# Decoder layer on one core: operands of two quarters in one load, small transfers joined, output products spread, DVE in program order

## The chip, the cores and the metric

One core of a Trainium2 chip runs the whole program in one launch. The metric is device time in microseconds, from the first to the last instruction with what lies around them. The engines are PE (matrix products), DVE (vector), ACT (activations and scaled copies), POOL (elementwise) and SP, which here only issues transfers between main memory and the on-chip memory. Products land in the PSUM banks, of which there are eight.

## The reference

Eight sequences of 512 tokens with 256 features pass through three sublayers, each followed by a layer norm without gains.

```python
x = _layernorm(x + _L0_attn_ref(x, w_qkv, w_proj))           # self-attention, 16 heads of 16, rotary
x = _layernorm(x + _L0_xattn_ref(x, ctx_1024, ctx_1024, Wq, bq, Wk, bk, Wv, bv, Wo, bo))  # cross-attention, 16 heads
x = _layernorm(x + _L0_ffn_ref(x, wqkv, q_scale, k_scale, wo, ln_g, ln_b, w1, b1, w2, b2))
```

The third sublayer is itself a stack of two layers, each with local attention in windows of 128 tokens (8 heads of 64, unit-length queries and keys, a rotary table with a decay, a look at the window before) and a gated network of 682 hidden features after a layer norm:

```python
for l in range(2):
    x = _layer(x, wqkv[l], q_scale[l], k_scale[l], wo[l], ln_g[l], ln_b[l], w1[l], b1[l], w2[l], b2[l])
```

All is float32. The kernel gets this accuracy by writing each operand as a high part and a low part in a shorter format and adding three products (high by high, high by low, low by high).

## The kernel before

**Stages.** Sixteen items (`seq`: eight sequences of self-attention, then eight of cross-attention) take four quarters each, a quarter being four heads. They are the first stage, 64 quarters. Then come 64 windows of local attention (two layers of 32), with the gated network's halves (`half`) between them.

**Who sets the order.** Each function registers pieces of work with a planned time: `pe(...)` for products, `at(...)` at a time, `af(...)` so long after a product. `tq(q, g, u)` is the planned start of quarter q (plus g quarters and u sixteenths of it), with `TQ` microseconds to a quarter. `trace()` replays the plan, taking a PSUM bank's reuse as `GAP` behind its last product, sorts all pieces by time and emits them. `ORDERED` names the engines whose instructions are tied to this order (PE and ACT). For DVE, POOL and SP a scheduler beneath chooses, after the first microseconds. Each engine and each transfer queue works through its own list strictly in order, so what waits holds up what stands behind it.

**A quarter** (`quarter`). `fill` brings the operands of four heads from main memory (`dh`) into a half of `kA` or `kB` (keys) and one of four `Qst` tiles (queries), as four transfers of 192 KB. Two quarters ahead, sixteen products `pss` give scores whose row maxima DVE takes (`mx`, tile `nm`). `nhl` on POOL splits the maxima in two parts, `pm` on PE transposes them, ACT copies them (`mhl`) and two small transfers (`mq`) set them as two more rows under the queries, so that sixteen more products `pst` give scores less maximum, transposed. ACT takes their exponentials (`ex`, tile `pt`), and products `po` with the values and a column of ones give output and sums. On PE this is a chain of blocks: four `pst` and four `pss`, four `po`; in the middle of each block stands a filler.

**Fillers** are the products of other items: queries and keys (`project`, three products at a time), values (`values`, six), and the output projection (`end`, tile `pp`, six). They share one PSUM bank, "m". Their places are given by the numbers `K0`, `K1`, `Q0`, `Q1`, `V0`, `V1`, `E0` and `E1` in sixteenths of a quarter from the item's first quarter. An output projection of one half (256 tokens) is followed by two adds on DVE (`res`), statistics, a reciprocal root on ACT and POOL, a scaled copy and a store.

**Normalizing** (`norm`). ACT copies `po` to `ob`, SP stores it (`od`). Every second quarter `norm` runs six parts, at `n0` to `n5` microseconds after the last `po`: load of sums (`sm`) and outputs (`OTr`), reciprocal on DVE (`rs`), its way through main memory (`rd`, `R`), a multiplication and a split on POOL.

**Weights of the windows** (`pre_weights`, `pre`). Beside cross-attention 34 tiles are loaded (`f_w`), split on POOL and stored in two transfers (`spl`); `fetch` brings them back later. `small_loads`, `xp_load` and `xp_scale` bring biases, gains, scales and the rotary tables `xp` and multiply the tables by the scales. `low_zeros` writes zeros under the low key parts `kLA` and `kLB`, which serve only the windows.

Of the kernel before, what the change touches and what calls it, by code (L numbers as in the profile page):

```python
# [10 lines left out]
F32 = mybir.dt.float32  # L11
# [16 lines left out]
NC2 = 72  # L28
TQ = 13.05
TW = 13.49  # L30
GAP = 0.7
# [4 lines left out]
    'hne': 1, 'fne': 1, 'nw4': 1, 'gce': 0, 'f2': 1.5, 'f3': 2.514, 'E0z': 120, 'E1z': 124, 'nd': 3,  # L36
    'phx': 0, 'psf': 2.0, 'np': 2, 'nhe': 1, 'pa': 9.182, 'pb': 36.0, 'pst0': 0.75, 'pr': 4.9,
    'px0': -6.0, 'px1': 0.5, 'pcut': 8.255, 'wvt': 8.0, 'wpt': 50.0, 'v0': 5.801, 'pmz': 3.4, 'acq':
    0.543, 'trt': -0.482, 'so_': 0, 'ld': 0.024, 'ct': -0.049, 'ath': 0.3, 'acp': 0.34, 'ra': 1.2,
    'rb': 3.612, 'c0': 6.101, 'c1': 0.771, 'cl': 0.9, 'sh': 1.043, 'sl': 3.159, 'avc': 0.269, 'rs':  # L40
    0.001, 'rb_': -0.03, 'ead': 0.4, 'est': 1.802, 'fi': 0.202, 'mh': 0.122, 'md': 1.2, 'mq': 4.283,
    'ob': 0.522, 'od': 1.2, 'n0': 4.069, 'n1': 7.425, 'n2': 8.487, 'n3': 11.192, 'n4': 14.127, 'n5':
    14.896, 'wl': 0.698, 'sp': 1.2, 'spl': 0.8, 'wr': 0.299, 'ws': -0.192, 'h1': 6.196, 'hb': 6.5,
    'hh': 0.422, 'hl': 1.056, 'LB': 1, 'x1': 9.0, 'rk': 7.466, 'rq': 6.0, 'sd': 17.807, 'pt':
    18.326, 'nw': 6, 'bx': 3, 'en': 2, 'ea': 0.404, 'eb': 0.722, 'pvg': 1, 'run': 2, 'phe': 0,
    'xke': 1, 'ohe': 1, 'pvn': 4, 'trx2': -0.174, 'q2': 0.027, 'k2': -0.077, 'v2': 0.0, 'tq2':
    -0.215, 'tk2': -0.339, 's2': 0.137, 'p2': 0.011, 'w2': 0.186, 'm2': 0.043, 'mn': 7, 'K0': -100,
    'K1': -92, 'Q0': -84, 'Q1': -76, 'V0': -56, 'V1': -48, 'E0': 124, 'E1': 132, 'T0': -120, 'T1':
    -92, 'nh': 1.6, 'pm': 7.854, 'mp': 0, 'trx': 0.61, 'xh': 0.93, 'xl': 2.343, 'q': 0.307, 'k':
    -0.038, 'sq': -0.05, 'sum': 1.287, 'rn': 3.235, 'un': 3.706, 'r0': 4.857, 'r1': 5.838, 'v':  # L50
    0.585, 'vc': 0.574, 'tq': 0.119, 'tk': -0.15, 'qh': 0.659, 'ql': 1.085, 's': 0.406, 'ds': 0.111,
    'ma': -0.055, 'so': 1.814, 're': 2.218, 'no': 4.347, 'p': 0.056, 'dp': 0.174, 'pc': 0.514, 'pv':
    0.201, 'oh': -0.155, 'ol': 1.273, 'w': 0.192, 'dw': 0.083, 'wa': 0.94, 'th': 0.761, 'g0':
    -0.359, 'g1': 1.888, 'm': 0.375, 'dm': 0.095, 'mad': -0.105, 'pe': 6, 'ne': 13, 'h': 0.618, 'f':
    0.484, 'mx': -0.083, 'ex': 0.488, 'pq0': 0, 'pq1': 5, 'lq': 22.263, 'ldq': 3.16, 'pcd': 3.053,
    'sq_': 0, 'pst': 8.62, 'nw1': 1, 'nw3': 1, 'nd1': 0.437, 'ne1': 0.395, 'nd3': 0.525, 'tp':
    -0.271, 'tpd': -0.102, 'lw1': 1.125, 'lw2': 0.37,
}
P.update({'ws': 0.5, 'T1': -100, 'trt': 0.2})

# [3 lines left out]
def tile_decoder(  # L64
# [5 lines left out]
    f_w, f_qs, f_ks, f_gb, f_b1, f_b2,  # L70
# [11 lines left out]
    drp = ctx.enter_context(tc.tile_pool(name="drp", bufs=3, space=DRAM))  # L82
    dr1 = ctx.enter_context(tc.tile_pool(name="dr1", bufs=1, space=DRAM))
# [68 lines left out]
    ORDERED = ("PE", "Activation") + ("SP",) * P['so_']  # L152
# [17 lines left out]
    def trace():  # L170
# [49 lines left out]
        steps.sort(key=lambda s: s[:3])  # L220
        for t, _, _, fn in steps:
            fn()
            ins = nc.cur_bb.bb.instructions
            for i in ins[seen[0]:]:
                e = str(i.engine).split(".")[-1]
                if e not in ORDERED and t > T0 + P['pt']:
                    continue
                if e in last:
                    tc.add_manual_dep(
                        i, last[e],  # L230
                        mybir.DependencyInfo(mybir.DependencyClass.NoSync, mybir.DependencyReason.DATA),
                        reason="order",
                    )
                last[e] = i.name
            seen[0] = len(ins)
# [123 lines left out]
    NST = 4  # L359
    kA, kB, kLA, kLB = [stk.tile([128, NW, 4, 128], F32R, name=f"kT{i}") for i in range(4)]  # L360
    Qst = [stk.tile([128, 2, N], F32R, name=f"Qst{i}") for i in range(NST)]
# [18 lines left out]
    def setup_keys():  # L380

        for k in (kA, kB):
            for r in (48, 112):
                dma(k[r:r + 2].rearrange("p w g n -> p w (g n)").bitcast(F32),
                    ones.unsqueeze(1).to_broadcast([2, NW, N]))
# [13 lines left out]
    def att_weights(kind, t0, dt):  # L399
# [4 lines left out]
        for c in range(2):  # L404
            r = slice(c * 128, c * 128 + 128)
            if kind == 0:
                parts = lambda r=r: [(lambda f: f, s_wqk[r])]
            else:
                parts = lambda r=r: [(lambda f: f[:, :256], c_wq[r]), (lambda f: f[:, 256:], c_wk[r])]
            load_split(t0 + c * dt, "wqk", parts, le, W, ("qk", c), q=qs[c])  # L410
        for n, (key, src) in enumerate((("v", (s_wv, c_wv)[kind]), ("p", (s_wp, c_wo)[kind]))):
            hook = None
            if kind == 1 and key == "p":
                hook = out_bias
            load_split(t0 + (2 + n) * dt, "w" + key,
                       lambda src=src: [(w2d, src.rearrange("(c p) m -> p c m", p=128))],
                       lv, W, key, q=qs[n], hook=hook, **({} if kind else {"dt": P[('wvt', 'wpt')[n]]}))
# [348 lines left out]
    def quarter(q):  # L766
# [3 lines left out]
        Q = Qst[q % NST]  # L770
        Sq = {}

        def fill():
            ks = (kA, kB)[q // 2 % 2].rearrange("p w g n -> p (w g n)")
            Kt[q] = [ks[:, (q % 2 * 2 + g) * N:(q % 2 * 2 + g) * N + N] for g in range(2)]
            behind("dh", i, 0, 4 if q else 0)
            for t, d in ((ks[:, q % 2 * 2 * N:q % 2 * 2 * N + 2 * N], dhs[1]), (Q.rearrange("p g n -> p (g n)"), dhs[0])):
                for e in range(2):
                    dma(t[e * 64:e * 64 + 48].bitcast(F32).rearrange("p (g n) -> p g n", g=2),
                        d[i % ND][4 * qd + e:4 * qd + 4:2].rearrange("g r n -> r g n"))  # L780
            Sq["nm"] = sp.tile([128, 4, NW], F32, name="nm", tag="nm")

        at(tq(q - 3, 2, P['fi']) if q else T0 + 13.0, fill)


# [40 lines left out]
        def mq():  # L826
            m = Sq.pop("mhl")
            for par in range(2):
                dma(Q[par * 64 + 48:par * 64 + 50].bitcast(F32).rearrange("r g (c n) -> r (g c) n", c=NW),
                    m[par * 16:par * 16 + 16])  # L830
# [49 lines left out]
        af(e_, P['od'], od)  # L880
        if qd % 2:
            for part, d in enumerate((P['n0'], P['n1'], P['n2'], P['n3'], P['n4'], P['n5'])):
# [28 lines left out]
    def xp_load(l):  # L911
# [3 lines left out]
        for j, s in enumerate((f_qs[l:l + 1], f_ks[l:l + 1])):  # L915
            t = W["xp"][j].rearrange("p (t w d) -> p t w d", t=2, w=NW)
            dma(qk[:, 2 * j], s.to_broadcast([128, 64]))
            dma(qk[:, 2 * j + 1, 0:32], s[:, 32:64].to_broadcast([128, 32]))
            dma(qk[:, 2 * j + 1, 32:64], s[:, 0:32].to_broadcast([128, 32]))
            for a in range(2):  # L920
                dma(t[:, a], t_xp[2 * j + a].rearrange("(w p) d -> p w d", p=128))
# [21 lines left out]
    def pre(t, l, key, load, gain=None, tail=False):  # L943
# [4 lines left out]
        def cut(part):  # L948
# [5 lines left out]
            elif part == 1:  # L954
                h, lo = st["h"] = c2("wsh", F32R), c2("wsl", F32R)
                nc.gpsimd.tensor_copy(h, f)
            else:
                h, lo = st["h"]
                sub(nc.gpsimd, lo, f, h)

        def store():
            dma = (dma_, dma_g)[P['sq_']]
            h, lo = (a.bitcast(F32) for a in st.pop("h"))
# [7 lines left out]
            else:  # L971
                dma(d[0], h)
                dma(d[1], lo)
# [29 lines left out]
    def pre_weights():  # L1003
        n = NL * len(TILES)
        ta, tb = tq(4 * B + P['pq0']), tq(8 * B - P['pq1'])
        for l in range(NL):
            at(tq(4 * B) if l == 0 else tq(4 * B, 1), held(lambda l=l: small_loads(l)))
# [16 lines left out]
    def small_loads(l):  # L1024
        W = MW[l]
        gb = W["gb"] = const.tile([128, 2, 2], F32, name=f"gb{l}")
        dma(gb, f_gb[l])
        b1 = W["b1"] = const.tile([128, 11], F32, name=f"b1{l}")
        dma(b1, f_b1[l])
        b2 = W["b2"] = const.tile([128, D], F32, name=f"b2{l}")  # L1030
        dma(b2, f_b2[l:l + 1].to_broadcast([128, D]))
# [335 lines left out]
    def half(hb):  # L1367
# [97 lines left out]
        def gate(c, part):  # L1465
# [14 lines left out]
            if c < 4:  # L1480
                u = Qst[c].rearrange("p g n -> p (g n)")[:, hb % 2 * N:hb % 2 * N + N]
# [95 lines left out]
    at(T0 + 60.0, low_zeros)  # L1577
# [16 lines left out]
def layout(inputs):  # L1594
# [22 lines left out]
    for k, n in (("f_qs", "q_scale"), ("f_ks", "k_scale"), ("f_b2", "b2")):  # L1617
        a[k] = f(g["L0_ffn_" + n])
    nl = a["f_b2"].shape[0]
# [17 lines left out]
    a["f_gb"] = f(np.stack([g["L0_ffn_ln_g"], g["L0_ffn_ln_b"]], 1).reshape(nl, 2, 2, 128).transpose(0, 3, 1, 2))  # L1637
# [7 lines left out]
    a["f_b1"] = b1  # L1645
# [13 lines left out]
    for m in (sc, 1.0 / sc):  # L1659
        tb.append(np.concatenate([c * m, c * m], axis=1))  # L1660
        tb.append(np.concatenate([-s * m, s * m], axis=1))
    a["t_xp"] = np.stack(tb).astype(np.float32)
# [7 lines left out]
         "c_bv", "c_bo", "f_w", "f_qs", "f_ks", "f_gb", "f_b1", "f_b2", "t_cs", "t_xp", "t_mask"]  # L1670
# [17 lines left out]
```

## Time and profile before

| | |
|---|---|
| median of three runs | 2227.28 us (2225.7 to 2239.14) |
| profiled execution | 2240.65 us, its span 2238.9 us |
| mean granted clock of PE | 0.966 |
| PE busy | 2134.8 us, 95% |
| ACT, DVE, POOL busy | 1687.5, 1648.9, 1469.2 us |
| moved by transfers | 324.92 MB, mean 145 GB/s |
| time per quarter, between `pm` products | 12.6 to 23.8 us from the ninth quarter to the fifty-eighth, 11.2 where no filler stands |

The profile shows one execution. Busy shares are means over stages that differ: what a hole in an engine is worth must be read in its stage. A line of the timeline gives start, duration, engine, source line, operation, the tiles that it writes and reads, how many, and in brackets how long the engine stood idle before it and what ended that. Many products are issued from one helper (L244), so they are told apart by tiles. "PEld" is the loading of the standing operand, which runs beside PE. A PE that is busy is not a PE at its peak, and its speed depends on the granted clock.

### The profile page before, as it was taken

The page shows a single profiled execution, that of the slowest core. Times are in us where ns is not written, and L with a number is a line of the kernel's source. Part 1 is how long each engine was busy: PE and PEld are TensorE (multiplying, and loading weights), DVE is VectorE, ACT ScalarE, POOL GpSimd, SP SyncE. Part 2 cuts the span into 40 slices and gives each one's busy share as a digit, 9 for nine tenths or more (in the row PEclk, how much of TensorE's full clock was granted, in tenths as well). Part 3 has the DMA queues.
Part 4 walks back from the last instruction along what each step waited for, and adds up shares of the span by engine and source line. Part 5 has one row for each costly group of instructions (what it writes and reads, how often), then busy time and mean ns, then how long its engine had stood idle before and what let it go on. Part 6 is the DMA issues. An engine that isn't in the chain of part 4 may idle for free.

```text
span 2238.9 us, 46438 instructions
## 1 busy us (share of the span) xinstructions
PE 2134.8 (95%) x15016; PEld 1528.5 (68%) x15016; DVE 1648.9 (74%) x4126; ACT 1687.5 (75%) x4087; POOL 1469.2 (66%) x2052
## 2 busy tenths in 40 slices
PE   8999999999999999998999999999999999999996
PEld 6434444444444444367889999998989898989986
DVE  4878888877787768826777777776777777777773
ACT  2778888877787778846878777787777878787874
POOL 5276666324565546347777777777778888888874
PEclk7899999999999999979999999999999999999998
DMA  7566666656778777555433333334453333333331
GB/s 185 147 204 182 196 191 197 197 163 207 225 248 252 243 251 244 175 152 153 120 84 86 86 89 87 84 86 136 105 165 88 96 94 89 87 97 91 92 89 42
DMA packets 249734, 324.92 MB, mean 145 GB/s; under 512 B 41756, under 2 KB 131956, under 8 KB 249492
## 3 DMA queue, kind: packets, MB, share of 16 engines
q1 hardware_dynamic: 248788, 320.90, 50.4%
q8 instruction: 121, 1.98, 0.4%
q10 hardware_dynamic: 704, 1.05, 0.1%
q14 instruction: 121, 0.99, 0.1%
HBM read 156.24 MB, written 110.36 MB: 119 GB/s over the span
## 4 chain that ended last, share of the span: by engine, by line
PE 74%; DMA 9%; ACT 6%; POOL 5%; DVE 4%; issue 2%; SPq 1%; POOLq 0%; ACTq 0%; DVEq 0%
PE pga L244 11%; PE pst L244 10%; PE po L853 10%; PE pqkv L244 9%; PE pqk L244 4%; PE po L244 4%; PE pss L244 4%; PE py L244 4%; PE plo L1300 4%; PE pls L244 3%; PE ptp L1284 3%; PE pv L244 2%; PE ptr L1179 2%; DMA hs<-xd 2%; PE pp L244 2%
## 5 line engine op out<-in xcount | busy, mean ns | idle before, releaser
L796 DVE TENSOR_REDUCE nm<-pss 128x1 f32<-128x512 f32 x1024 | 653.2, 683 | 194.7 <-PE pss L244 152.5
L845 ACT ACTIVATE pt<-pst 128x512 f32<-128x512 f32 x1024 | 556.8, 602 | 139.1 <-PE pss L244 87.0
L244 PE MATMUL pst<-Qst,kT 50*128 50x512 f32 x1024 | 392.7, 461 | 22.7 <-ACT pt L845 13.7
L244 PE MATMUL pss<-kT,Qst 48*128 48x512 f32 x1024 | 399.3, 470 | 11.4 <-DVE nm L796 8.8
L244 PEld LDWEIGHTS pst<-Qst,kT 50*128 50x128 f32 x1024 | 164.5, 191 | 278.3 <-ACT pt L845 212.1
L244 PE MATMUL pqkv<-fwqh,xwT 128*128 128x512 f32 x768 | 311.7, 414 | 1.4 <-ACT pt L845 1.4
L853 PE MATMUL po<-pt,Vst 128*32 128x512 f32 x2048 | 284.1, 628 | 0.0
L1248 ACT ACTIVATE ms<-ms,n 128x256 f32<-128x256 f32 (+1 forms) x512 | 241.2, 473 | 41.7 <-DVE n L1240 36.2
L244 PE MATMUL pga<-hTh,w1h 128*128 128x256 f32 x704 | 204.1, 290 | 0.3 <-ACT hTh L1426 0.3
L1144 POOL TENSOR_TENSOR rT<-qn,xp 128x256 f32<-128x256 f32 x256 | 182.7, 735 | 31.6 <-DVE qn L1134 22.5
L244 PE MATMUL pga<-hTl,w1h 128*128 128x256 f32 x704 | 200.1, 284 | 1.5 <-DVE hTl L266 1.4
L1259 POOL TENSOR_TENSOR ms<-ms,lrs 128x512 f32<-128x512 f32 (+1 forms) x192 | 180.6, 947 | 31.1 <-DVE lrs L1254 24.8
L1240 DVE CUSTOM_DVE_ANT_0 ms<-pls,mask 128x256 f32<-128x256 f32 (+1 forms) x512 | 175.5, 383 | 33.4 <-PE pls L244 31.3
L244 PE MATMUL pga<-hTh,w1l 128*128 128x256 f32 x704 | 199.2, 283 | 0.0
L244 PEld LDWEIGHTS pss<-kT,Qst 48*128 48x128 f32 x1024 | 165.6, 192 | 28.5 <-DVE nm L796 20.4
L1474 ACT ACTIVATE gg<-pga,b 128x256 f32<-128x256 f32 (+1 forms) x192 | 91.2, 475 | 120.9 <-PE pga L244 117.5
L244 PE MATMUL pls<-kT,qs 128*128 128x256 f32 (+1 forms) x1024 | 168.8, 287 | 5.4 <-DVE n L1240 2.8
L1151 POOL TENSOR_TENSOR qn<-qn,xp 128x512 f32<-128x512 f32 x128 | 165.2, 1291 | 10.0
L1153 POOL TENSOR_TENSOR qn<-qn,rT 128x512 f32<-128x512 f32 x128 | 165.3, 1291 | 9.9
L244 PEld LDWEIGHTS pqkv<-fwqh,xwT 128*128 128x128 f32 x768 | 148.1, 193 | 24.1 <-ACT pt L845 2.4
L244 PE MATMUL pqkv<-fwql,xwT 128*128 128x512 f32 x384 | 154.1, 401 | 0.0
L244 PEld LDWEIGHTS pls<-kT,qs 128*128 128x128 f32 x1024 | 142.1, 192 | 11.1 <-issue 2.8
(172 smaller groups left out, 5502.9 us busy)
## 6 DMA issues: line engine op xcount, KB each, us to landing
kT<-kh SPq DMA_DIRECT2D x256, 128.0 KB
dh<-phi SPq DMA_DIRECT2D x60, 512.0 KB
kT<-dh SPq DMA_DIRECT2D x128, 192.0 KB
Qst<-dh SPq DMA_DIRECT2D x128, 192.0 KB
od<-ob SPq DMA_DIRECT2D x64, 256.0 KB
kT<-kl SPq DMA_DIRECT2D x128, 128.0 KB
dh<-plo SPq DMA_DIRECT2D x60, 256.0 KB
wst<-f_w SPq DMA_DIRECT2D x46, 256.0 KB
```

Source lines behind the costliest of these rows:

```text
L244: nc.tensor.matmul(out_, a, b_, start=i == 0, stop=i == n - 1)
L796: nc.vector.tensor_reduce(Sq["nm"][:, hh, qc:qc + 1], Sq.pop(("s", u)), AX.X, ALU.max, negate=True)
L845: nc.scalar.activation(p, Sq.pop(("t", hh)), AF.Exp, scale=scale)
L853: nc.tensor.matmul(po[hh * 32:hh * 32 + 32, :], V[kc][:, h * 17:h * 17 + 32], Sq.pop(("p", kc, hh)), start=kc == 0, stop=kc == NW - 1)
L1144: nc.gpsimd.tensor_tensor(h8(T2)[:, :, a * 32:a * 32 + 32], h8(qn)[:, :, 32 - a * 32:64 - a * 32], xp[:, 1, w:w + 1, a * 32:a * 32 + 32].t ...
L1151: nc.gpsimd.tensor_tensor(h8(qn), h8(qn), xp[:, 0, w:w + 1].to_broadcast([128, 8, 64]), ALU.mult)
L1153: nc.gpsimd.tensor_tensor(qn, qn, R.pop(("T2", j)), ALU.add)
L1240: nc.vector.tensor_tensor_reduce(ms[:, m, :nk], ps[:, m, :nk], FW[0]["mask"][:, 256 - nk:], -8.0, 3.0e38, ALU.add, ALU.min, n8[:, m:m + 1])
L1248: nc.scalar.activation(ms[:, m, :nk], ms[:, m, :nk], AF.Exp, bias=n8[:, m:m + 1], scale=-1.0, accum_out=sm[:, m:m + 1])
L1259: nc.gpsimd.tensor_tensor(pr[:, :, :nk], pr[:, :, :nk], rs.unsqueeze(2).to_broadcast([128, 2, nk]), ALU.mult)
L1300: nc.tensor.matmul(po[par * 64:par * 64 + 64, g * 128:g * 128 + 128], V[:, h * 64:h * 64 + 64], PT[:, par, c], start=c == 0, stop=c == nch ...
L1474: nc.scalar.activation(S["g", c][:rows], gin, AF.Gelu, bias=gb)
```

## The change

Operands: the four loads of a quarter become four of 384 KB for a pair of quarters (from the third quarter on), and there are three places for a pair instead of two. `kLA` and `kLB` serve as keys and queries of the third, and so `low_zeros` moves from the start to the end of the first stage.

Small transfers: the two stores of a split weight become one (from a tile of its own in a pool `wsp`; the common pool shrinks from 72 to 68 tiles), and biases, gains, scales and rotary tables are laid out by the host so that 26 small loads become 8.

Output products: `E0` and `E1` go from 124 and 132 to 108 and 124, and the K, Q and V places and other planned times move with them. Splitting of the window weights begins at quarter 15.4 instead of 32.

Order: DVE is tied to the program's order until the last quarter of the first stage (`do_` 1); the reciprocal and its neighbours are planned later (`n0` to `n5`), except for the last item.

```diff
-TQ = 13.05
+TQ = 12.91
-GAP = 0.7
+GAP = 0.49
...
-    ... 'ob': 0.522, 'od': 1.2, 'n0': 4.069, 'n1': 7.425, 'n2': 8.487, 'n3': 11.192, 'n4': 14.127, 'n5': 14.896
-    ... 'K0': -100, 'K1': -92, 'Q0': -84, 'Q1': -76, 'V0': -56, 'V1': -48, 'E0': 124, 'E1': 132, 'T0': -120, 'T1': -92
+    ... 'ob': 0.522, 'od': 1.367, 'n0': 5.72, 'n1': 9.555, 'n2': 10.595, 'n3': 13.85, 'n4': 18.602, 'n5': 22.869
+    ... 'K0': -108, 'K1': -100, 'Q0': -92, 'Q1': -76, 'V0': -60, 'V1': -52, 'E0': 108, 'E1': 124, 'T0': -112, 'T1': -100
+    ... 'pqa': 0.482, 'do_': 1, 'po_': 0
...
-    ORDERED = ("PE", "Activation") + ("SP",) * P['so_']
+    ORDERED = ("PE", "Activation")
+    ORDERED_A = ORDERED + ("SP",) * (P['so_'] == 1) + ("DVE",) * (P['do_'] == 1) + ("Pool",) * (P['po_'] == 1)
...
-                if e not in ORDERED and t > T0 + P['pt']:
+                if e not in (ORDERED_A if t < t_att else ORDERED) and t > T0 + P['pt']:
...
-    Qst = [stk.tile([128, 2, N], F32R, name=f"Qst{i}") for i in range(NST)]
+    Qst = [stk.tile([128, 4, N], F32R, name=f"Qst{i}") for i in range(2)]
+    KR = [t.rearrange("p w g n -> p (w g n)") for t in (kA, kB, kLA)]
+    QR = Qst + [kLB.rearrange("p w g n -> p (w g n)").rearrange("p (g n) -> p g n", n=N)]
...
         def fill():
-            for t, d in ((ks[:, q % 2 * 2 * N:q % 2 * 2 * N + 2 * N], dhs[1]), (Q.rearrange("p g n -> p (g n)"), dhs[0])):
-                for e in range(2):
-                    dma(t[e * 64:e * 64 + 48].bitcast(F32).rearrange("p (g n) -> p g n", g=2),
-                        d[i % ND][4 * qd + e:4 * qd + 4:2].rearrange("g r n -> r g n"))
+            n = 1 if q < 2 else 2
+            lo, hi = q % 2 * 2, q % 2 * 2 + 2 * n
+            for t, d in ((KR[r].rearrange("p (g n) -> p g n", n=N), dhs[1]), (QR[r], dhs[0])):
+                for e in range(2):
+                    dma(t[e * 64:e * 64 + 48, lo:hi].bitcast(F32),
+                        d[i % ND][4 * qd + e:4 * qd + 4 * n:2].rearrange("g r n -> r g n"))
...
-        at(tq(q - 3, 2, P['fi']) if q else T0 + 13.0, fill)
+        if q < 2 or q % 2 == 0:
+            at(tq(q - 3, 2, P['fi']) if q else T0 + 13.0, fill)
+        at(tq(q - 3, 2, P['fi']) if q else T0 + 13.0, begin)
...
-        for j, s in enumerate((f_qs[l:l + 1], f_ks[l:l + 1])):
-            t = W["xp"][j].rearrange("p (t w d) -> p t w d", t=2, w=NW)
-            dma(qk[:, 2 * j], s.to_broadcast([128, 64]))
-            dma(qk[:, 2 * j + 1, 0:32], s[:, 32:64].to_broadcast([128, 32]))
-            dma(qk[:, 2 * j + 1, 32:64], s[:, 0:32].to_broadcast([128, 32]))
-            for a in range(2):
-                dma(t[:, a], t_xp[2 * j + a].rearrange("(w p) d -> p w d", p=128))
+        dma(qk.rearrange("p t d -> p (t d)"), f_qk[l:l + 1].to_broadcast([128, 256]))
+        for j in range(2):
+            dma(W["xp"][j], t_xp[j])
...
-                dma(d[0], h)
-                dma(d[1], lo)
+                dma(d.rearrange("a p n -> p a n"), hl)
...
-        ta, tb = tq(4 * B + P['pq0']), tq(8 * B - P['pq1'])
+        ta, tb = tq(4 * B * P['pqa'] + P['pq0']), tq(8 * B - P['pq1'])
...
-    at(T0 + 60.0, low_zeros)
+    at(tq(4 * L - 4, 2), low_zeros)
```

## The prediction

> **What bounds the kernel now.** I read the page first, then busy time by stretches, then the timeline of each engine around every hole in PE.
>
> ```profile
> span 2238.9 us, 46438 instructions
> PE 2134.8 (95%) x15016; PEld 1528.5 (68%) x15016; DVE 1648.9 (74%) x4126; ACT 1687.5 (75%) x4087; POOL 1469.2 (66%) x2052
> PEclk7899999999999999979999999999999999999998
> ```
>
> PE bounds it; the others stand at 66 to 75%. So a change can pay in two ways only: fewer holes in PE, or fewer stretches at a lower granted clock. By stretches (us, then busy time of PE, PEld, DVE, ACT, POOL, then granted clock, DMA share, GB/s):
>
> ```profile
> 134.00:450.00 316.00, 309.19 (x1916) 134.94 (x1914) 256.32 (x450) 259.02 (x531) 190.46 (x265) 1.00 0.66 194
> 450.00:892.00 442.00, 417.01 (x2474) 187.69 (x2472) 329.04 (x583) 338.37 (x686) 222.40 (x351) 0.95 0.74 229
> 892.00:985.00 93.00, 84.79 (x478) 38.04 (x474) 54.13 (x104) 65.58 (x135) 37.17 (x53) 0.94 0.62 181
> 985.00:1080.00 95.00, 84.43 (x562) 72.79 (x559) 56.45 (x196) 60.23 (x182) 62.73 (x93) 0.87 0.52 146
> 1080.00:1540.00 460.00, 455.57 (x3707) 420.62 (x3705) 351.60 (x1070) 361.12 (x981) 349.38 (x445) 1.00 0.34 86
> 522.40:532.70 10.30, 10.10 (x38) 4.16 (x39) 5.42 (x10) 3.71 (x7) 4.12 (x6) 0.50 0.68 221
> ```
>
> Self-attention (134 to 450) runs at full clock, cross-attention (450 to 892) at 0.95, the window stage from 1080 on has 1% of holes. The loss is in cross-attention and at the seam behind it. The last line shows what a hole costs besides itself: after one, the clock is 0.50 for about 10 us. The hole and its makers, from the timelines:
>
> ```profile
> 514.50 0.33 SPq L238 DMA_DIRECT2D od<-ob  x1
> 519.46 0.66 SPq L238 DMA_DIRECT2D sm<-od  x1
> 521.64 0.35 DVE L692 RECIPROCAL rs<-sm 128x32 f32<-128x32 f32 x1 [3.87 <-DMA sm<-od]
> 522.60 0.79 PE L244 MATMUL pss<-kT,Qst 48*128 48x512 f32 x1 [3.30 <-DVE nm L796]
> ...
> 728.99 0.64 SPq L238 DMA_DIRECT2D sm<-od  x1
> 730.34 0.68 SPq L238 DMA_DIRECT2D Qst<-mhl  x1
> 734.30 0.76 PE L244 MATMUL pst<-Qst,kT 50*128 50x512 f32 x1 [1.72 <-DMA Qst<-mhl]
> ...
> 513.96 0.39 PE L244 MATMUL pv<-wvh,xkh 128*128 128x256 f32 x1 [0.94 <-DVE res L724]
> ```
>
> First: DVE stands at a reciprocal whose sums have not landed, the maxima queue behind it, no PSUM bank comes free, PE stops. Second: SP stands at `sm`, which waits for its store `od`, and the maxima `mhl` for the next quarter queue behind. Third: a values product waits for DVE to empty the one bank "m" that an output product has just filled.
>
> **The change, part by part.**
>
> *Output products apart.* E1 moves from 132 to 124 sixteenths of a quarter, E0 from 124 to 108, the K, Q and V products with them. In the built program every block of four score products now carries exactly one filler; before, one block in sixteen carried the second E1 product and a V product together and one carried none. The 13 items with such a meeting show a hole of 0.85 to 0.95 us each: 13 x 0.9 = 11.7. The levelling: quarter steps between `pm` products in self-attention are 12.57 (243.13 to 255.70, the one with the empty block) and 15.09, sum 27.66; less the hole 26.76; two even quarters cost 13.15 and 13.41, sum 26.56; so 0.2 x 13 = 2.6. Moved along with E: two adds, the statistics, POOL's small Newton steps and the `xd` stores; they are the same in number and now lie a quarter earlier, not between the two most crowded blocks. Sum -14, bounds 0 (another wait takes the place) and -16.
>
> *DVE in program order, reciprocal later.* `n1` goes from 7.425 to 9.555 us behind the last `po`, the `sm` load from 4.07 to 5.72. Before, the built order has a reciprocal behind 58 to 62 maxima counted from its quarter, now behind 64 (66 to 68 in four places; the last two of all are as before), so 2 to 6 maxima of 0.65 us later: 1.3 to 3.9 us. Its waits here were 2.87, 3.87 and 4.95 us at 455, 521 and 583. Behind a waiting reciprocal stand the maxima, and behind those PE. Holes 1.14 + 3.30 + 3.22 = 7.7; half clock after them 10.2 + 10.2 + 6.8 us (found by narrowing the stretches), half of it lost: 13.6. Sum -21, bounds 0 and -21. A strict order could add waits of its own; what else DVE takes there (`res`, statistics, `xql`) follows products of PE whose order is fixed too, so I charge nothing, and a rival takes it up.
>
> *Small transfers joined, pairs loaded together.* SP issues 1718 transfers instead of 1890: 128 + 128 operand loads become 132, 72 weight stores 40, 26 small rows 8, and two rows of ones come in. At 0.4 us an issue (median of the operand loads 0.38 and 0.43) that is 69 us of SP's time, none on the path itself. What counts is the order: in the built program both `mhl` transfers of a quarter now precede `sm` in nearly all quarters of cross-attention, where before `sm` stood ahead in every second. Holes on `mhl` 0.73 + 1.72 + 1.70 + 1.68 = 5.8, half clock after two of them (6.8 + 10.2)/2 = 8.5. Sum -14, bounds 0 and -14. Both half-clock sums make 22.1, and 0.05 x 442 from the stretch's row is 22.1 as well.
>
> *Larger loads.* A pair comes as four transfers of 384 KB instead of eight of 192, for 31 pairs. No row shows one; a 256 KB store lands within 2.05 us in a calm moment (`od` at 307.95, `sm` issued at 310.00) and 4.96 us in a crowded one (514.50 to 519.46). By bytes, 3.1 to 7.4 us. The plan gives half a quarter, 6.45 us; in the built order the last of the four stands ahead of the `od` that closes the quarter before its use, some 10 us, since the third slot is free earlier. I take 0; bounds 0 and what rival A says. The Trainium skill, "DMA: Bandwidth & Descriptors", section "Anatomy of one DMA", gives a fixed part of about 2.0 us plus the bytes at 436 GB/s; estimated from that page a pair's transfer would land in 2.9 us, a quarter's in 2.45, so it also says 0; the crowded row above is twice as long as this page allows, so it does not close the case.
>
> *Moved loads and POOL work.* Weight splitting starts at quarter 15 instead of 32: 34 times a load, 0.61 and 1.28 us on POOL (12 with 1.04 more), 77 us, of which some 29 fall into self-attention: POOL there goes from 190 to about 220 of 316 us, 70%. `nhl` on POOL has about 5 us between its planned place and `pm`. Nothing, up to +6. The zero rows (two 512 KB transfers) go to the end of attention, behind the `mhl` of that quarter: nothing. Two buffers for the split halves, each needed for about 16 us (by the plan, first split to store) of the 33 that two starts lie apart: nothing. The early hole of 2.15 us at 114, with 0.69 and half of 10.2 us behind it, 7.9, may go or stay, as early transfers shift; I take 0.
>
> *Layer seam.* Ten issues from 1528.16 to 1534.07 become three, in rows of 2 KB instead of 256 bytes.
>
> ```profile
> 1528.16 1.46 SPq L238 DMA_DIRECT2D qk<-f_qs  x3
> 1535.34 1.44 POOL L928 TENSOR_TENSOR xp<-xp,qk 128x256 f32<-128x256 f32 x2 [5.35 <-DMA xp<-t_xp]
> 1544.01 0.90 PE L1179 MATMUL ptr<-ident,qn 128*128 128x128 f32 x3 [4.37 <-POOL qn L1153]
> ```
>
> Some 4.5 us less on SP, and the hole is 4.37 with 6.8 us of half clock: 7.8. I take -7, bounds 0 and -8.
>
> *Seam behind attention* (892 to 1080). Lost now: 0.06 x 93 + 0.13 x 95 = 18 in clock, 11 in holes. The same seven issues go from between 946 and 952.5, ahead of the last `mhl` and `od`. Most of the rest is the last sequence's chain, which stays. -6, bounds +5 and -15.
>
> **Sum.** -14 - 21 - 14 - 7 - 6 = -62 against the profiled run: 2240.65 - 62 = 2179. That run lies 13.4 above the median of 2227.28; I suppose that half of these 13.4 us are stalls of the same kind, which the median run did not have to give back: 2227.3 - 62 + 6.7 = 2172.
>
> On the clock: the Trainium skill, "TensorE: Matmul & The Clock Gate", section "HAM oscillation", warns of idle gaps of PE above about 3.4 us. Here gaps of 1.14, 1.70 and 1.72 us were followed by half clock already (one of 1.68 was not). By the page no hole of 134 to 892 would cost clock, and the sum would be 22 us smaller, 2194; the row decides.
>
> **Rivals.**
> A, pair loads land late (slower). Place: first `pss` of an even quarter. Four transfers are 1.57 MB; at cross-attention's mean of 229 GB/s they take 6.9 us, more than the planned 6.45. It decides from a landing more than 10 us behind issue. Price, for the 16 pairs of cross-attention: a hole of 1.7 and half of 6.8 us lost clock, 5.1 each, 82 in all: 2254, slower by 1.2%. For: DMA at 0.74 there. Against: no `pss` waits for DMA in steady state now, total bytes are the same, slots are free earlier.
> B, waits change place: a strict DVE finds other late inputs, and the 35 us of the two middle parts stay: 2207, within 1%. For: `od` itself was issued up to 6 us late at 508. Against: that came from SP's crowd, which thins.
> C, only the fillers help, and ACT or DVE bound the quarter: no, since a quarter without fillers takes 11.2 us against 13.2, so they have room; 2227 - 14 = 2213 if so.
>
> **How the numbers follow.** Forecast 0.77, A 0.09, B 0.09, C 0.05. Forecast alone 2145 to 2203: all bounds taken, the early hole too, give 2227 - 16 - 21 - 14 - 8 - 15 - 8 = 2145; half of the middle parts' 35 staying gives 2190, both seams' 13 staying 2203. With B and C the range is 2145 to 2213. One per cent (22 us) is about what a measurement can tell from none: faster by more 0.80, within 0.11, slower 0.09.
>
> **What would show it.** Right: quarter steps between `pm` near 13.2 in self- and 13.6 in cross-attention with no 15 or 22; clock 1.00 through cross-attention; no `pv` waiting for `res`, reciprocals without waits; no hole at the layer seam. Wrong: `pss` waiting for the operand loads, `sm` or reciprocals still waiting ahead of maxima, or a clock below 0.97 from 134 to 850.

## The result and the profile after

The changed kernel takes 2244.5 us (median of 20 runs, 2230.9 to 2254.3) against 2231.9 us for the kernel before beside it: ratio 1.0047, 95% interval 1.0029 to 1.0065. Slower by half a per cent, where 2172 was forecast. The profiled execution, the slowest of the twenty, has a span of 2252.2 us. Head of its page, then the same stretches as in the prediction (us, busy time of PE, PEld, DVE, ACT, POOL, then granted clock, DMA share, GB/s):

```profile
span 2252.2 us, 46192 instructions
PE 2135.8 (95%) x15016; PEld 1530.3 (68%) x15016; DVE 1655.9 (74%) x4126; ACT 1685.3 (75%) x4087; POOL 1466.9 (65%) x2052
PEclk8999989998899989978999999999999999999998
```

```profile
134.00:450.00 316.00, 296.71 (x1789) 129.72 (x1781) 240.52 (x424) 244.52 (x500) 198.08 (x278) 0.96 0.75 208
450.00:892.00 442.00, 413.40 (x2449) 187.67 (x2447) 330.06 (x578) 331.58 (x676) 203.69 (x327) 0.93 0.77 210
```

The shares of the engines hardly moved; the clock did. Self-attention, at 1.00 before, is granted 0.96, and cross-attention 0.93 instead of 0.95. Something makes holes in PE, now in both.

The page's groups and the timelines say what. These are the groups of `pst` products (idle time before them at the end, then what ended most of it), first of the kernel before, then of the changed one. Its row holds the 704 products whose operands lie in `Qst`; the other 320, whose operands lie in `kLA` and `kLB` (`kT` in the profile), have 18.6 us, so that 22.7 us have become 56.4.

```profile
L244 PE MATMUL pst<-Qst,kT 50*128 50x512 f32 x1024 | 392.7, 461 | 22.7 <-ACT pt L845 13.7
L254 PE MATMUL pst<-Qst,kT 50*128 50x512 f32 x704 | 273.0, 468 | 37.8 <-DMA Qst<-mhl 29.6
```

SP's timeline around one hole, then ACT's and PE's:

```profile
491.18 0.43 SPq L248 DMA_DIRECT2D kT<-dh  x1
491.70 0.91 SPq L248 DMA_DIRECT2D res<-x  x2
492.70 0.42 SPq L248 DMA_DIRECT2D rd<-rs  x1
493.17 0.42 SPq L248 DMA_DIRECT2D kT<-dh  x1
501.78 0.60 SPq L248 DMA_DIRECT2D R<-rd  x1
502.47 0.79 SPq L248 DMA_DIRECT2D od<-ob  x1
503.31 0.42 SPq L248 DMA_DIRECT2D kT<-dh  x1
503.82 0.96 SPq L248 DMA_DIRECT2D xr<-xd  x2
504.88 0.89 SPq L248 DMA_DIRECT2D wst<-ctxT  x2
505.86 1.39 SPq L848 DMA_DIRECT2D Qst<-mhl  x2
```

```profile
498.82 0.26 ACT L843 COPY mhl<-pm 32x128 f32<-32x128 f32 x1
```

```profile
511.77 0.76 PE L254 MATMUL pst<-Qst,kT 50*128 50x512 f32 x1 [6.17 <-DMA Qst<-mhl]
```

SP issues nothing from 493.6 to 501.8: it stands at the load `R`, which reads the 16 KB store `rd` that was issued at 492.70. The maxima `mhl` are ready at 499.1 and are issued only at 505.9 and 506.6, behind `R`, `od`, an operand load and four other loads. PE runs out of work at 505.6, and the maxima land 4.5 us behind the end of their issue. So a quarter can bear `mhl` only some 0.6 us late (505.6 less 499.1, less 1.4 of issuing and 4.5); here it is 6.8 late, and the difference is the hole. This happens once an item, behind the normalization of its first half.

In the kernel before, `R` stood ahead of the next maxima as well, in every half of an item, but it was issued before they were ready:

```profile
489.72 0.46 SPq L238 DMA_DIRECT2D rd<-rs  x1
493.87 0.60 SPq L238 DMA_DIRECT2D R<-rd  x1
498.54 1.41 SPq L238 DMA_DIRECT2D Qst<-mhl  x2
498.09 0.26 ACT L824 COPY mhl<-pm 32x128 f32<-32x128 f32 x1 [0.37 <-PE pm L819]
```

In the mean of the thirteen first halves from 130 to 900 us, `R` was issued 5.1 us before the maxima were ready, and in the change 0.5 us after. Of these 5.6 us, 3.1 come from `rd`, issued 9.2 us ahead of the ready maxima before and 6.1 now, and 2.5 from the time between the issues of `rd` and `R`, 4.1 us before and 6.6 now. A further part of the delay lies between `R` and the maxima: the change plans the loads of the next item's input (`xr`, `wst`) half a quarter earlier (`ld` and `ct` -8 instead of 0.024 and -0.049), and in twelve of these thirteen halves they now stand ahead of the maxima, where before they came behind them. At the hole shown they take 2.0 of the 6.8 us; no run moved them back.

SP's own waits from 100 to 950 us (us in total, times, longest), the kernel before first, then the changed one:

```profile
SPq L238 <- DMA od<-ob: 37.2, 18, 4.4
SPq L238 <- DMA rd<-rs: 14.0, 16, 2.1
```

```profile
SPq L248 <- DMA rd<-rs: 109.4, 28, 8.1
SPq L248 <- DMA od<-ob: 5.5, 6, 2.0
```

The wait for `od` that the change was to remove has gone, from 37.2 to 5.5 us; a wait of 109.4 for `rd` has come. Its price in PE, from its timeline: eleven holes of 1.13 to 6.17 us on `mhl`, 43 us, and with nine of them 85 us of half clock. Some 16 us of this half clock lie inside the holes; half of the rest, 35 us, is lost: 78 us together, by this estimate. Without them the span would be 2174 us.

By stage, from the starts of the `pm` products in PE's timeline (us; the ninth quarter opens the second column):

| kernel | to the 9th quarter | 20 quarters, self | 28 quarters, cross | rest, to the last product |
|---|---|---|---|---|
| before | 160.1 | 276.0 | 427.5 | 1367.7 |
| changed | 144.2 | 292.8 | 435.8 | 1372.1 |

So the start gained 16, and the rest gave it back twice.

### The profile page after: what moved, and what is told of

The parts are those of the page before. It is cut to its first block, busy times and chain, and to the rows that moved or that the text cites. A ratio compares the mean times of both kernels' runs of the same rounds, so it can differ in the third digit from the quotient of the medians.

```text
span 2252.2 us, 46192 instructions
## 1 busy us (share of the span) xinstructions
PE 2135.8 (95%) x15016; PEld 1530.3 (68%) x15016; DVE 1655.9 (74%) x4126; ACT 1685.3 (75%) x4087; POOL 1466.9 (65%) x2052
## 4 chain that ended last, share of the span: by engine, by line
PE 76%; DMA 7%; ACT 7%; POOL 5%; DVE 3%; issue 2%; SPq 0%; POOLq 0%; DVEq 0%; ACTq 0%
PE pga L254 11%; PE pst L254 10%; PE po L872 10%; PE pqkv L254 9%; PE po L254 4%; PE pqk L254 4%; PE plo L1316 4%; PE pss L254 4%; PE py L254 3%; PE pls L254 3%; PE ptp L1300 3%; PE pv L254 2%; PE ptr L1195 2%; DMA Qst<-mhl 2%; PE pp L254 2%
## 5 line engine op out<-in xcount | busy, mean ns | idle before, releaser
L254 PE MATMUL pst<-Qst,kT 50*128 50x512 f32 x704 | 273.0, 468 | 37.8 <-DMA Qst<-mhl 29.6
L254 PE MATMUL pss<-kT,Qst 48*128 48x512 f32 x704 | 276.8, 477 | 2.3 <-DMA Qst<-dh 1.2
L254 PEld LDWEIGHTS pst<-Qst,kT 50*128 50x128 f32 x704 | 113.7, 194 | 210.9 <-ACT pt L864 143.9
L1490 ACT ACTIVATE gg<-pga,fb 128x256 f32<-128x256 f32 (+1 forms) x192 | 91.0, 474 | 122.8 <-PE pga L254 117.8
L254 PE MATMUL po<-w2h,Qst 128*128 128x256 f32 x512 | 142.9, 309 | 6.8 <-DVE xwr L1361 5.6
```

The source lines that it names most:

```text
L254: nc.tensor.matmul(out_, a, b_, start=i == 0, stop=i == n - 1)
L1490: nc.scalar.activation(S["g", c][:rows], gin, AF.Gelu, bias=gb)
```

## The experiments

All edits are to the changed kernel unless said otherwise. "`rd` to `R`" is the mean time between the two issues in SP's timeline, from 130 to 900 us.

**Is it the transfers ahead of `rd`?** Residual loads a quarter earlier:

```diff
-    'rs': 0.001
+    'rs': -16.0
```

> The changed kernel with one number altered: the two loads of the residual (512 KB in all) are planned a quarter earlier, so that they no longer stand just ahead of the small store rd of each item's first half. Theory T (SP stands at R, which waits for rd; rd lands 6.5 to 9.1 us after its issue because it queues behind the residual loads and the 384 KB operand loads; the mhl transfers behind R are late, PE stops for 4 to 6 us and runs at half clock afterwards): rd to R falls to 3 to 5 us in the first halves as it is in the second halves, most of the eleven holes on mhl (43 us, with 44 us lost to half clock) go, about 2175 us. Rival U (the reciprocals are simply planned too late, whatever queues ahead of rd): R still comes after mhl is ready, 2230 to 2245 us.

2221.5 us, 0.9941 [0.9910, 0.9972]. `rd` to `R` in first halves 4.7 us (6.6 in the change), SP's wait for `rd` 79.5 us, holes on `mhl` of 0.98 to 6.53 still there. Some 23 us of the loss, not the 70 that were expected.

**Is it the times of the normalization?**

```diff
-    'n0': 5.72, 'n1': 9.555, 'n2': 10.595, 'n3': 13.85, 'n4': 18.602, 'n5': 22.869, 'od': 1.367
+    'n0': 4.069, 'n1': 7.425, 'n2': 8.487, 'n3': 11.192, 'n4': 14.127, 'n5': 14.896, 'od': 1.2
```

> The changed kernel with the six normalizing steps and the od store planned as before (od 1.2, n0 4.069, n1 7.425, n2 8.487, n3 11.192, n4 14.127, n5 14.896); DVE still in program order. T: R is reached some 2.7 us earlier, the transfers behind it wait that much less, the holes on mhl fall from 4-6 to 1-3 us each: about 2200 us. U: all of the loss was the later reciprocals, 2165 to 2180 us. Rival V (early reciprocals make DVE wait in program order, which the later times had cured): waits of reciprocals for sm of 1 to 4 us per item come back, 2230 us or more.

2240.2 us, 1.0020 [0.9985, 1.0055]: no gain clear of the noise. But most of the holes now have another cause. POOL's, ACT's and PE's timelines of this kernel:

```profile
506.46 1.29 POOL L714 TENSOR_TENSOR OTr<-OTr,R 128x512 f32<-128x512 f32 x1 [5.43 <-DMA R<-rd]
...
510.83 0.20 POOL L354 TENSOR_TENSOR lno<-lnm,lnrs 128x2 f32<-128x2 f32 x1
```

```profile
511.06 1.09 ACT L366 ACTIVATE res<-res,lno,lnrs 128x256 f32<-128x256 f32 x2 [4.67 <-POOL lno L354]
```

```profile
512.68 0.79 PE L255 MATMUL pst<-Qst,kT 50*128 50x512 f32 x1 [4.12 <-ACT pt L865]
```

The multiplication now stands on POOL before its `R` has landed; the small Newton steps are queued behind it, ACT stands at its scaled copy, the exponentials `pt` behind that, and PE. `R` late is paid in either place: on SP in the change, on POOL here.

**Is it the size of the loads?** One quarter a load, the three places kept:

```diff
-            n = 1 if q < 2 else 2
+            n = 1
...
-        if q < 2 or q % 2 == 0:
-            at(tq(q - 3, 2, P['fi']) if q else T0 + 13.0, fill)
+        at(tq(q - 3, 2, P['fi']) if q else T0 + 13.0, fill)
```

> The changed kernel with the operands of each quarter loaded by themselves again (four transfers of 192 KB a quarter), but still in three places. T: half of the operand bytes that stand around rd are loaded in another quarter; rd to R falls by 1.5 to 3 us, the holes by as much, about 2205 us. Rival W (the size of the pair loads is the whole cause): holes gone, 2165 to 2180 us. U: no change, 2240 us.

2185.7 us, 0.9774 [0.9731, 0.9817]: 59 us of the loss, and most of the forecast. `rd` to `R` in first halves 4.1 us, SP's wait for `rd` 44.2; four holes on `mhl` stay, 3.01, 3.67, 3.70 and 1.63 us, all between 260 and 444 us.

**Or the burst?** The pair's moment kept, each transfer in two halves:

```diff
-                    dma(t[e * 64:e * 64 + 48, lo:hi].bitcast(F32), ...)
+                    for j in range(n):
+                        dma(t[e * 64:e * 64 + 48, lo + 2 * j:lo + 2 * j + 2].bitcast(F32), ...)
```

> The changed kernel with the loads of a pair kept at the pair's moment, but each 384 KB transfer split into two of 192 KB, one for each quarter of the pair. Theory of the burst (1.57 MB put into the queues at once, whatever the transfers' size): as the changed kernel, holes on mhl of 1 to 6 us once an item, 2235 to 2250. Rival, the size of one transfer (a small store behind one 384 KB transfer waits longer than behind 192 KB): rd to R falls from 6.3 to 7.1 us to 4 to 5 us and the time to 2185 to 2205.

2228.7 us, 0.9984 [0.9955, 1.0013]: both theories have a half right. SP's wait for `rd` falls to 43.0 us, as with single loads, but SP's timeline shows what fills the time:

```profile
495.04 0.34 SPq L248 DMA_DIRECT2D rd<-rs  x1
...
500.43 0.60 SPq L248 DMA_DIRECT2D R<-rd  x1
501.08 2.34 SPq L248 DMA_DIRECT2D kT<-dh  x5
503.46 0.94 SPq L248 DMA_DIRECT2D xr<-xd  x2
504.88 1.38 SPq L248 DMA_DIRECT2D wst<-ctxT  x2
507.05 1.75 SPq L849 DMA_DIRECT2D Qst<-mhl  x2
```

`R` is issued 5.4 us behind `rd` instead of 9.1, but five operand loads instead of one now stand between it and the maxima, which go out 5.4 us late (hole 5.06). What is late is the maxima: the size of a transfer sets how long SP stands, the number of loads behind `R` how far back the maxima are.

**Is it DVE's order?**

```diff
-    'do_': 1
+    'do_': 0
```

> The changed kernel with DVE's order left to the scheduler as before (do_ 0). T: DVE is not the cause; SP's list is the same and so are the holes on mhl: 2235 to 2250 us. Rival V (program order on DVE costs time): 2220 us or less.

2240.2 us, 1.0041 [1.0011, 1.0071]: holes in the same places. The order of DVE has no part in the loss that shows.

**The direct test: `R` behind the maxima, all else as in the change.**

```diff
-    'n3': 13.85, 'n4': 18.602, 'n5': 22.869
+    'n3': 19.5, 'n4': 22.6, 'n5': 23.5
```

> The changed kernel with pair loads and residual loads as they are, and the load R planned 5.65 us later (n3 19.5, with n4 22.6 and n5 23.5 behind it): in the built order R now stands behind od and both mhl transfers instead of ahead of them. Theory (what costs is SP standing at R with mhl queued behind it, not the slow landing itself): no hole on mhl over 1 us from 250 to 900 us, rd to R of 8 us or more without a price, and 2160 to 2185. Rival (the DMA engines themselves are late, so mhl lands late wherever R stands, or POOL's product waits for R in turn and holds up the small steps behind it): holes stay, 2215 to 2250.

2195.4 us, 0.9867 [0.9810, 0.9925]. SP's wait for `rd`:

```profile
SPq L249 <- DMA rd<-rs: 0.2, 1, 0.2
```

49 us back for a changed place in SP's queue, with every transfer as large as before (40 us when each kernel is set against the kernel before in its own rounds). So most of the loss is SP standing at `R` with the maxima behind it. Holes on `mhl` of 0.96 to 4.55 us remain in six places, so the time is above the forecast of this run: something of the pair loads' price stays.

**How much do the pair loads cost by themselves?** Three combinations with early residual loads: single loads; pair loads with `R` behind the maxima; single loads with `R` behind the maxima.

> The changed kernel with two edits together: operand loads of one quarter each (192 KB, three places kept) and the residual loads a quarter earlier (rs = -16). Theory: the four holes left with single loads (3.02, 3.67, 3.71, 1.63 us at 260 to 442) come from the two 256 KB residual loads that stand ahead of the small store rd; with both away SP waits for R no longer than 3 to 4 us, at most one hole on mhl over 1 us stays, and the time is the single-load time 2185.7 less 12 us of holes and 15 us of half clock: 2155 to 2168. Rival (the residual loads matter only beside pair loads, since SP's wait before R is set by the distance from the reciprocal): the four holes stay and the time is 2180 to 2190.

> The changed kernel with its pair loads, R behind the maxima (n3 19.5, n4 22.6, n5 23.5) and the residual loads a quarter earlier (rs = -16). Theory (pair loads are harmless once nothing urgent stands behind a wait for rd): the holes left in cross-attention (1.84, 1.21, 0.97 us) go, and the time falls from 2195.4 to that of single loads with early residual loads, 2165 to 2178. Rival (pair loads keep a price of their own, mhl landing late behind 384 KB transfers): holes on mhl of 1 to 3 us stay and 2183 to 2197.

> Single loads, early residual loads and R behind the maxima (n3 19.5, n4 22.6, n5 23.5): the run with pair loads that gave 2189.0, but with 192 KB loads of one quarter. Theory (pair loads have a price of their own): as single loads with R ahead, 2165 to 2178. Rival (R's late place costs the 16 us, because POOL's product, planned 4 us later, and the split OTh run into the output products or the next maxima): 2182 to 2195.

| | pair loads | single loads |
|---|---|---|
| `R` ahead of the maxima | 2221.5 | 2172.6, 0.9718 [0.9677, 0.9758] |
| `R` behind the maxima | 2189.0, 0.9811 [0.9758, 0.9864] | 2164.7, 0.9701 [0.9674, 0.9728] |

With `R` behind, pair loads cost 24 us; with `R` ahead, 49. The late place of `R` costs nothing: with single loads it is even 8 us better, though the intervals overlap. The expected 2165 to 2178 for pair loads was missed (holes on `mhl` of 1.0 to 3.2 us between 316 and 493), and why pair loads keep 24 us with no SP wait for `rd` was not taken apart further. In the two longest of these holes (3.23 us at 378 and 1.96 at 494) the maxima are issued 1.2 and 0.6 us after they are ready, and PE goes on 6.2 and 5.9 us behind the end of their issue, against 4.5 in the hole shown first: there it is more the landing that is late than the issue. The lower right kernel is the best of all, 3.0% faster than before. Its page and its 20 and 28 quarters, then the same two stretches of the kernel before:

```profile
span 2159.8 us, 46377 instructions
PE 2090.7 (97%) x15016; PEld 1508.6 (70%) x15016; DVE 1652.1 (76%) x4126; ACT 1682.2 (78%) x4087; POOL 1467.1 (68%) x2052
PEclk9999999999999999989999999999999999999998
```

```profile
143.96:415.35 271.39, 269.48 (x1677) 118.62 (x1673) 224.51 (x395) 227.46 (x467) 185.70 (x256) 1.00 0.73 221
415.35:796.98 381.63, 379.81 (x2384) 173.27 (x2380) 318.79 (x561) 322.75 (x659) 198.66 (x317) 1.00 0.79 240
```

```profile
160.14:436.18 276.04, 269.47 (x1677) 118.31 (x1673) 223.74 (x395) 226.62 (x466) 167.10 (x237) 1.00 0.65 192
436.18:863.63 427.45, 403.51 (x2384) 180.69 (x2380) 317.44 (x561) 326.34 (x658) 211.34 (x331) 0.95 0.73 228
```

The 28 quarters of cross-attention go from 427.5 to 381.6 us at full clock: 22 us less idle time, and 24 us less busy time for the same 2384 products, since none runs at half clock. DMA's share is higher (0.79) than in the change (0.77), at 240 GB/s against 210: bandwidth was not what was short in the change.

**Can the pair be loaded elsewhere?** The pair beside the first half's normalization 10 us later (the other 3.2 later), without and with early residual loads, and 6 us earlier with them:

```diff
-            at(tq(q - 3, 2, P['fi']) if q else T0 + 13.0, fill)
+            at(tq(q - 3, 2, P['fi']) + (10.0 if q % 4 == 2 else 3.2) * (q > 2) if q else T0 + 13.0, fill)
```

> The changed kernel with 384 KB pair loads, but the pair that is loaded around the first half's normalization planned 10 us later (the other 3.2 us later): its four transfers now stand behind R and both mhl transfers instead of two ahead of R and two between R and mhl. Theory (it is the meeting of the pair's 1.57 MB with rd, R and mhl that costs, not the size of a transfer): rd to R in first halves 4 to 5.5 us, mhl late by under 1.5 us, and 2175 to 2200, as with single loads. Rival (pair loads cost wherever they stand, since whatever they meet, here the stores dh and the sums sm, is late in turn): holes in the next quarters instead, 2220 to 2250.

> The same with the residual loads a quarter earlier as well (rs = -16), so that neither stands near rd. Theory: what single loads with early residual loads gave, 2172.6, and its 36 us a pair of fewer issues bring nothing: 2165 to 2185. Rival, as above: 2200 to 2235.

> Pair loads, early residual loads, R ahead of the maxima as in the change; the pair loaded around the first half's normalization is planned 6 us earlier, so that in the built order all its four transfers stand ahead of rd or R and only small and weight transfers between R and the maxima. Theory (the meeting costs: the two loads behind R and the one behind rd): 2175 to 2200, holes on mhl under 2 us. Rival (1.15 to 1.57 MB ahead of rd delay its landing still more): rd to R over 6 us, holes of 3 to 6 us as in the change with early residual loads, 2215 to 2235.

Later: 2357.4 us, 1.0574 [1.0528, 1.0620], and 2354.3, 1.0557 [1.0505, 1.0609]. This was a mistake in the design: the plan has half a quarter between a pair's load and its first `pss`, so that 10 us later is too late. SP's timeline and PE's:

```profile
511.59 1.74 SPq L248 DMA_DIRECT2D kT<-dh  x2
513.38 0.92 SPq L248 DMA_DIRECT2D Qst<-dh  x2
```

```profile
522.07 0.76 PE L254 MATMUL pss<-kT,Qst 48*128 48x512 f32 x1 [8.87 <-DMA Qst<-dh]
```

It still gives the price of a pair that nothing hides: `pss` goes on some 10 us behind the first issue and 8 us behind the last, once an item. `rd` to `R` did fall, to 3.7 and 3.2 us in first halves.

Earlier: 2228.4 us, 0.9975 [0.9944, 1.0006], no better than pair loads in the change's place with early residual loads (2221.5). More bytes now stand ahead of `rd`: `rd` to `R` is 7.2 us in first halves, against 4.7, and SP's wait for it 81.0 us. So of the places tried none serves the pair: ahead of `rd` it delays `R`, and later it is itself late.

**What are the other terms worth?** The single-load kernel with early residual loads, with DVE left free:

```diff
-    'do_': 1
+    'do_': 0
```

> Single loads, early residual loads, and DVE no longer held to the program's order (do_ = 0), the reciprocal's late place kept. It prices the DVE order alone where nothing else hides it. Theory (what removes the DVE waits is the later reciprocal and the sums that land in time; the strict order itself is worth little): 2168 to 2180, as with the order, 2172.6. Rival (the strict order is worth the 21 us that the prediction gave it): 2185 to 2200 with holes of pss behind a reciprocal.

2180.2 us, 0.9784 [0.9738, 0.9829], against 0.9718 [0.9677, 0.9758] with the order: the intervals overlap. The 20 and 28 quarters take 279.3 and 381.1 us, with the order 280.7 and 380.6. The strict order brings nothing that shows in these quarters; what differs lies behind them.

The kernel before with its values products 4 sixteenths of a quarter later, so that none meets an output product:

```diff
-    'V0': -56, 'V1': -48
+    'V0': -52, 'V1': -44
```

> The kernel before with one edit: the V products 4 sixteenths of a quarter later (V0 -52, V1 -44), so that in the built order no block of four score products carries both an output and a values product, and none of the sixteen is empty. Nothing of the rest of the change is in it. This is the first term of the prediction by itself, -14 (13 holes of 0.9 us on pv behind res, and 0.2 us of levelling each): 2213 to 2221 against a before of 2232, ratio 0.993 to 0.995, no pv waiting for res. Rival (the values wait only changes place): no gain, ratio 0.998 to 1.002, other holes in place of the 13.

2229.9 us, 0.9993 [0.9965, 1.0020]: the rival. The holes of `pv` are gone, but in cross-attention five of 0.97 to 4.21 us on `pss` behind DVE's `xql` have come, and one item of self-attention (four quarters) hardly moves. Kernel before, this one, and the best one:

```profile
201.48:255.70 54.22, 53.11 (x337) 23.14 (x333) 44.34 (x79) 44.57 (x93) 34.43 (x48) 1.00 0.64 188
```

```profile
202.47:256.57 54.10, 53.62 (x336) 23.29 (x332) 44.32 (x79) 44.76 (x92) 34.23 (x48) 1.00 0.63 188
```

```profile
183.95:237.09 53.14, 53.14 (x337) 23.10 (x333) 44.59 (x79) 44.89 (x92) 33.60 (x48) 1.00 0.65 190
```

Without the meeting, 1.1 us without work become 0.5, and PE is busy 0.5 us longer. With the output products in two groups of two, as in the change, the item has no hole and takes 1.08 us less than before; but the best kernel differs from the one before in much else, so that this is one comparison and no test of the grouping alone.

## Why the prediction was wrong, point by point

The single-load kernels show the forecast's gains nearly whole: 2172.6 and 2164.7 against 2172. What failed is the term taken at nothing, larger loads, and in the third term the order of SP's list, of which only one of two waits was looked at.

- *Larger loads, 0 (the failed step).* I asked whether a pair lands in time for its own `pss`. It does: in the change no `pss` of the steady state waits for `dh`. I did not ask what stands behind it in the same queue. With 384 KB loads and two residual loads of 256 KB issued close to it, the 16 KB store `rd` takes 6.6 us in first halves to release `R`, where it took 4.1. Measured price of the pair loads: 59 us in the change, 24 us in the best order. The 2.9 us estimated for a pair's transfer did not hold for four issued together either: where nothing hid them, `pss` started 10.5 us behind the first issue.
- *Small transfers, -14 (the failed step too).* I looked at whether both `mhl` transfers stand ahead of `sm`. They do, and the wait for `od` fell as forecast. I did not look at the other wait in SP's list, that of `R` for `rd`, with the next quarter's maxima behind it. They stood behind it before as well, and it did no harm while `R` was issued 5.1 us before they were ready. With the reciprocal planned 2.1 us later and `R` 2.7 (`n1`, `n3`), and with `rd` slower, it comes 0.5 us after, and the input loads that now stand between add to it. Putting `R` behind the maxima brought 40 to 49 us.
- *Output products apart, -14: right in size, as far as one item shows.* 1.08 us an item, times 13, is 14.0. The reason was half right at most: taking away the meeting with a values product brought nothing by itself. That the grouping of the output products brings it is argued, not tested alone.
- *DVE order and later reciprocal, -21.* No reciprocal waits for its sums in the changed kernel between 134 and 900 us (15.3 us in eight waits before). The 28 quarters of the best kernel are 45.8 us shorter; 21 + 14 from terms two and three and 7 x 1.08 are 42.6. The order's part in it is nothing within what was measured. The later reciprocal is not needed for it alone either: in the run with the times as before, no reciprocal waits between 134 and 900 us. SP's list, with the maxima ahead of `sm`, is common to these runs; what removes the waits was not taken apart.
- *Seams, -13 together.* Behind the cross-attention quarters the best kernel is 12.4 us shorter, the changed one 4.4 longer. From there to 1100 us the changed kernel has 51 us of half clock, the kernel before 37 and the best one 31. Why was not taken apart. At the layer seam the hole of 4.37 became two of 1.70 and 1.54, with no half clock.
- *The start, 0 with a bound of -8.* 16 us came in the changed kernel, and 10 to 17 in all that build on it but the two with the pair moved 10 us later: half clock ahead of the ninth quarter fell from 48 to 24 us. The zero rows that were moved out of the start may have to do with it; no run took it apart.
- *The rivals.* A had the right suspect and the wrong victim: it put the stall at the first `pss` of an even quarter. With a cost of 82 us for 16 stalls its size was near the 78 that came, which is luck, since the stall was another. B said that waits change place, but looked for them on DVE; they were on SP. Of the signs that I had named as "wrong", the clock came (0.94 from 134 to 850 us), the two waits did not, and none of them pointed at `R`.

The Trainium skill, "DMA: Bandwidth & Descriptors", section "Queues, rings and completion order", says that the increment that reports a transfer as landed is strongly ordered: it comes only after every earlier write of the same transfer engine. That is a rule I should have weighed: by it a small store cannot report before the writes of large transfers that stand ahead of it on its own transfer engines. The rows agree: `rd` to `R` is 1.6 us where no operand load was issued in the 3 us ahead (second halves, with the times as before), 3.0 (second halves) and 4.1 (first halves) with single loads, and 6.6 in the changed kernel's first halves. No run here tells this rule from transfers that merely wait their turn. The same page's "Rules for kernel authors" asks for transfers of 1 MiB and more for bandwidth; here twice the size cost 24 to 59 us, and bandwidth was not what was short: the single loads moved more, 240 GB/s against 210 in cross-attention.

## What to carry to other kernels

When a transfer is made larger, do not only ask when it lands: list what is issued behind it in the same queue, find the small stores that something waits for, and see what stands behind that waiting instruction. When a load that waits is planned later, or what it waits for gets slower, look up whether the urgent small transfer behind it is ready by then, and put the load behind that; a late `R` cost nothing here once nothing urgent stood behind it. The saved issues were worth nothing here: the best kernel is one with single loads.

## What the runs showed of the hardware

- From the issue of a 16 KB store to the issue of the load that reads it, 1.4 to 1.9 us passed where no operand load had been issued in the 3 us ahead (second halves, with the times as before), and 9.1 us with a 384 KB load and two residual loads of 256 KB in the 2 us ahead (the changed kernel at 492.70).
- Shares of DMA time say little of bandwidth: in the best kernel 0.79 of the engines' time moved 240 GB/s in cross-attention, in the changed one 0.77 moved 210.
- Holes of PE between 1 and 2 us are followed by half clock, but not always: 1.57 us (changed kernel) was followed by 3.4 us of it, 1.81 (single loads, early residual loads) by 6.8; in the run with `R` behind the maxima 1.22 by 10.2 and 1.77 by none. Of the eleven holes on `mhl` in the changed kernel nine had it, all of 1.57 us and more. In the longest it began inside the hole (mean granted clock 0.70 to 0.82 within four holes of 4.45 to 6.17 us), and the five of 4.45 to 5.75 us cost 7 to 11 us each in all, by the estimate above. Why holes of one size differ stays open.
